# Attention and a quantized convolution block: steps of issue moved, x of the first image on three queues, the constants' transfers behind it

## The chip, the cores and the metric

The kernel runs on one core of a Trainium2 chip. A core has a matrix engine (TensorE, PE in the profile; its weight loads are shown as PEld), a vector engine (VectorE, DVE), a scalar engine (ScalarE, ACT), GpSimd (POOL) and a queue engine (SyncE, SP). Each works through its own list of instructions in order and waits on semaphores for the others. Transfers (DMA) are issued by SyncE, ScalarE or GpSimd, each through its own queue. The metric is the time on the device in microseconds, the median of several runs. Before the change it is 2569.15 us (three runs: 2565.08, 2569.15 and 2569.88).

## The reference

Two layers, on x of four images, each of 128 channels and 64 x 64 points, in float32.

```python
# layer 0: attention over the 4096 points of an image, 4 heads of 32 channels
x_norm = _group_norm(x, norm_w, norm_b)          # 8 groups of 16 channels
qkv = einsum('oc,bchw->bohw', qkv_w, x_norm) + qkv_b
attn = softmax(einsum('bhid,bhjd->bhij', q, k) * 32 ** -0.5)
out = einsum('bhij,bhjd->bhid', attn, v)
x = x + einsum('oc,bchw->bohw', proj_w, out) + proj_b
# layer 1: two 3x3 convolutions with weights quantized to 3 bits
out = relu(batchnorm(conv3x3(x, lsq_quantize(w1, alpha1)), gamma1, beta1))
out = batchnorm(conv3x3(out, lsq_quantize(w2, alpha2)), gamma2, beta2)
x = relu(out + x)
```

The batch norms take mean and variance over all four images.

## The kernel before, in words

`_fast_body` does the work (a second, general path runs only if a bound on the softmax is broken, and it isn't run here).

*Start.* GpSimd fills a few small tiles and issues the loads of all constants (`column`, L95, and L115 to L127). x of the first image comes in eight chunks of 512 points on SyncE's and ScalarE's queues in turn (L590). Meanwhile `keep_warm` gives TensorE products that nobody reads. VectorE takes statistics of each chunk in order (`bn_stats`, L597); `norm_parts` turns them into the scale and the biases of the group norm, in steps zero to eight, with more `keep_warm` between. Then k, q and v of the first chunks are projected (L616). k and q are split into a high and a low part (`kst`, `qst`). Chunk 0 goes straight to its place (`direct`), the others are written to DRAM (`kd`, `qd`) and loaded again in the layout that the scores want (`load_k`, `load_q`).

*Attention.* There are 32 blocks: four images (b), eight blocks of 512 queries each (qb); n counts them all. A block runs over 32 steps kt of 128 keys, each in two halves. `scores` makes a half step of products (L442) and their exponential on ScalarE (L444) into a tile p; `weights` multiplies p with v into acc (L456) and VectorE adds p to a running sum r (L471). In six of the 32 steps (MOVED) the addition is done instead by a transfer of GpSimd's queue that adds into rm (L466), and at the end `merge` adds rm to r (L492). TensorE does three halves of scores, then three of weights, and so on (end of the attention, `run_scores` and `run_weights`). There are nine tiles for p, nine for k, three pairs of banks for scores and two banks for all else (acc, projections, sums).

*Side work.* Everything else is put between these halves by `schedule(n, before)`. It gives every piece a place: `at_half(p, f)` runs f after half p of the block, `add(kt, f)` after step kt, and `visit(i, first, second, evacuate)` uses the i-th end of a group of three (`ends[i]`), where TensorE changes from weights to scores. The place sets the order in each engine's list, not a time: an engine whose list has nothing else left runs ahead. Side work is: the end of the block before (`merge`; `sums` of r over the partitions; `spread`, `invert` and `gather`, which bring the sums to 16 columns, invert them and bring them back as rc by way of DRAM on SyncE's queue; `residual`, which loads x; `weigh`, which multiplies; `project`; `store`); the projections of chunks (in block 0 the rest of k and v of the first image and q of chunk 1, in block 1 the rest of q, later those of the next image); statistics and norm of the next image (`late`); the loads of the next k, v and q; and the quantization of the weights in `pieces`, whose first one of each third is a load on SyncE's queue.

*Convolutions.* The images are cut into bands of 16 rows. `load_band` loads one with its border, `split_band` makes its high and low part (L573, L574), `conv` takes 18 products for each half band. The first two bands are done while the last block is finished. `layer` runs over the bands and calls `prepare(m)` after band m, which is `first` in the first layer: it loads band m + 3 and splits band m + 2. The quantized weights of the second layer wait in DRAM (wqd) and are loaded into raw_w at L808, then copied at band 6.

Of the kernel before, what the change touches and what calls it, by code (L numbers as in the profile page):

```python
# [16 lines left out]
F32 = mybir.dt.float32  # L17
# [5 lines left out]
P = 128  # L23
# [55 lines left out]
def _fast_body(ctx, tc, x, norm_w, norm_b, qkv_wt, qkv_b, proj_wt, proj_b,  # L79
               w1, alpha1, gamma1, beta1, w2, alpha2, gamma2, beta2, out, cnt):  # L80
    nc = tc.nc
# [10 lines left out]
    const = ctx.enter_context(tc.tile_pool(name="const", bufs=1))  # L92
    small = ctx.enter_context(tc.tile_pool(name="small", bufs=2))

    def column(v, name):  # L95
        t = const.tile([P, 1], F32, name=name)
        nc.gpsimd.dma_start(out=t, in_=v.rearrange("(c o) -> c o", o=1))
        return t


# [11 lines left out]
    nc.gpsimd.memset(ones, 1.0)  # L112
    worst = const.tile([P, FB // D], F32, name="worst")
    nc.gpsimd.memset(worst, 0.0)
    nw, nb = column(norm_w, "nw"), column(norm_b, "nb")  # L115
    wqkv = const.tile([P, 3 * P], F32, name="wqkv")
    nc.gpsimd.dma_start(out=wqkv, in_=qkv_wt)
    bkq = const.tile([P, 2], F32, name="bkq")
    nc.gpsimd.dma_start(out=bkq[:, 0:1], in_=qkv_b[P : 2 * P].rearrange("(c o) -> c o", o=1))
    nc.gpsimd.dma_start(out=bkq[:, 1:2], in_=qkv_b[0:P].rearrange("(c o) -> c o", o=1))  # L120
    bv = const.tile([P, P], F32, name="bv")
    nc.gpsimd.dma_start(out=bv, in_=qkv_b[2 * P : 3 * P].partition_broadcast(P))
    wp = const.tile([P, P], F32, name="wp")
    nc.gpsimd.dma_start(out=wp, in_=proj_wt)
    bp = column(proj_b, "bp")
    bn = [(column(gamma1, "gamma1"), column(beta1, "beta1")),
          (column(gamma2, "gamma2"), column(beta2, "beta2"))]  # L127
# [102 lines left out]
    def x_chunk(b, j):  # L230
        return x[b].rearrange("c h w -> c (h w)")[:, j * FB : (j + 1) * FB]
# [74 lines left out]
    def keep_warm(count):  # L306

        t = psa.tile([P, FB], F32, name=f"idle{count}", tag="a")
        for _ in range(count):
            nc.tensor.matmul(t[:, 0:P], gavg, gavg, start=True, stop=True)  # L310
# [276 lines left out]

    halves = [ppool.tile([P, HEADS, FB], F32, name=f"xh{i}", tag="p") for i in range(2)]
    for j in range(NB):
        eng = (nc.sync, nc.scalar)[j % 2]  # L590
        eng.dma_start(out=halves[j // 4][:, j % 4, :], in_=x_chunk(0, j))
    table = const.tile([P, 1], F32, name="table")
    nc.scalar.activation(table, mhalf, AF.Exp)
    keep_warm(26)
    st = small.tile([P, NB, 6], F32, name="st0", tag="st")
    for j in range(NB):
        nc.vector.bn_stats(st[:, j, :], halves[j // 4][:, j % 4, :])  # L597
# [16 lines left out]
        load_v(b, j)  # L614

    for what, j in (("k", 0), ("q", 0), ("k", 1), ("v", 0), ("k", 2), ("v", 1), ("k", 3), ("v", 2),  # L616
                    ("v", 3)):
        for f in first_chunk(j, what, True):
            f()
        if what == "q":  # L620
            five_v()
            six_v()
        if what == "v" and j < 3:
            load_k(0, j + 1)


# [3 lines left out]
    def fetch(b, j):  # L630
        xin[b, j] = load_x(b, j)

    def schedule(n, before):
        b, qb = blocks[n]
        todo = []
        ends = [p for p in range(2 * NK - 2) if (2 * n * NK + p) % 3 == 2]
        two = b + 1 < B and qb in ((3, 4, 5) if b == 0 else (2, 3))

        def at_half(p, f):
            todo.append((p, f))  # L640

        def add(kt, f):
            todo.append((2 * kt + 1, f))

        def visit(i, first, second, evacuate=None, split=True):
            at_half(ends[i], first)
            e = ends[i + 1 if split else i]
            at_half(e, second)  # L650
            if evacuate:
                at_half(e + 1, evacuate)
            return e

        if before:
            add(1, before["merge"])
            e = visit(5 if two else 4 if n == 1 else 6, lambda: before["sums"](0), lambda: before["sums"](1),
                      split=not two and n != 1)
            at_half(e + 2, before["spread"])
            at_half(e + 6, before["invert"])  # L660
            at_half(e + 8, before["gather"])
            at_half(e + 12, before["residual"])
            at_half(ends[18] - 4, before["weigh"])
            at_half(ends[18], before["project"])
            at_half(ends[18] + 2, before["store"])
        if n + 1 < len(blocks):
            add(24 if n == 0 else 14, lambda: load_q(*blocks[n + 1]))
        if n == 0:
            for i, what, j in ((0, "k", 4), (2, "k", 5), (4, "v", 4), (6, "k", 6), (8, "v", 5),
                               (10, "k", 7), (12, "q", 1), (14, "v", 6), (16, "v", 7)):  # L670
                visit(i, *first_chunk(j, what, False), split=False)
                if what == "k":
                    at_half(ends[i] + 5, lambda j=j: load_k(0, j))
        if n == 0:
            for j in (2, 3):
                add(25 + j, lambda j=j: fetch(0, j))
        if n == 1:
            for i, j in zip((0, 2, 8, 10, 12, 14), range(2, NB)):
                if j > 3:
                    at_half(ends[i - 3], lambda j=j: fetch(0, j))  # L680
                visit(i, *project_parts(0, j, lambda j=j: xin[0, j])["q"], split=False)
        qn = qb if b else qb - 1
        if b + 1 < B:
            if qn == 1:
                st = small.tile([P, NB, 6], F32, name=f"st{b + 1}", tag="st")
                for j in range(NB):
                    add(3 * j // 2, lambda j=j: fetch(b + 1, j))
                    add(3 * j // 2 + 3, lambda j=j: nc.vector.bn_stats(st[:, j, :], xin[b + 1, j]))
                late[b] = norm_parts(b + 1, st)
                add(15, late[b][0])  # L690
                for i in (0, 1):
                    at_half(ends[13 + 2 * i], late[b][1 + 2 * i])
                    at_half(ends[13 + 2 * i] + 3, late[b][2 + 2 * i])
            if qn == 2:
                at_half(ends[1], late[b][5])
                at_half(ends[1] + 1, late[b][6])
                at_half(ends[1] + 1, late[b][7])
                at_half(ends[1] + 4, late[b][8])
            if b == 0:
                chunks = {2: (), 3: (0, 1), 4: (2, 3), 5: (4, 5), 6: (6,), 7: (7,)}  # L700
            else:
                chunks = {1: (), 2: (0, 1), 3: (2, 3), 4: (4,), 5: (5,), 6: (6,), 7: (7,)}
            for i, j in enumerate(chunks.get(qb, ())):
                p = project_parts(b + 1, j, lambda j=j: xin[b + 1, j])
                if not two:
                    for what, i in dict(k=1, q=10, v=13).items():
                        visit(i, *p[what])
                    continue
                for what, e in (dict(k=2, q=7, v=9) if i == 0 else dict(k=11, q=13, v=15)).items():
                    visit(e, *p[what], split=False)  # L710
                if i == 1:
                    add(8, lambda j=j: fetch(b + 1, j))
            if qn > 0 and qb + 1 in chunks:
                add(22, lambda j=chunks[qb + 1][0]: fetch(b + 1, j))
            if qb == NB - 1:
                for j in range(NB - 1):
                    add(4 * j + 1, lambda j=j: load_kv(b + 1, j))
        if b > 0 and qb == 0:
            add(1, lambda: load_kv(b, NB - 1))


        if b == B - 1 and qb < NB - 1:
            for kt in (1, 10, 20):
                add(kt, lambda: next(pieces, None))
        elif 0 < b and qb == 0:
            for kt in (1, 10, 15, 20, 25) + ((29,) if b == 1 else ()):
                add(kt, lambda: next(pieces))
        if n == len(blocks) - 1:
            add(5, lambda: load_band(0, 0))
            add(13, lambda: split_band(0, 0))  # L730
            add(17, lambda: load_band(0, 1))
            add(24, lambda: split_band(0, 1))
            add(27, lambda: load_band(0, 2))
        return sorted(todo, key=lambda t: t[0])
# [58 lines left out]
    last["residual"]()  # L793
    conv(ready[0, 0, 0], early[0][:, 1, :], 1, wq[0])
    split_band(*bandlist[2])
    last["sums_at_once"]()
    conv(ready[0, 0, 1], early[1][:, 0, :], 0, wq[0])
    conv(ready[0, 0, 1], early[1][:, 1, :], 1, wq[0])
# [6 lines left out]
    cv = [mid.tile([P, N], F32, name=f"cv{b}") for b in range(B)]  # L805
    raw_w = mid.tile([P, TAPS, P], F32, name="raw_w")
    wq.append(mid.tile([P, TAPS, P], F32R, name="wq1"))
    nc.sync.dma_start(out=raw_w, in_=wqd)  # L808


    a_q, a_g, a_n = ([small.tile([P, 1], F32, name=f"{n}{i}") for i in range(2)]
# [60 lines left out]
    def first(m):  # L872
        if m == 5:
            count_bad()
        if m == 6:
            nc.vector.tensor_copy(wq[1], raw_w)
        if m + 3 < len(bandlist):
            load_band(*bandlist[m + 3])
        if m + 2 < len(bandlist) and m > 0:
            split_band(*bandlist[m + 2])  # L880
# [527 lines left out]
```

## Time and profile before

| engine | busy us | share of the span |
|---|---|---|
| PE | 2515.2 | 98% |
| PEld (overlaps PE) | 1504.3 | 59% |
| DVE | 2137.1 | 83% |
| ACT | 2086.7 | 81% |
| POOL | 282.9 | 11% |

The span of the profiled run is 2567.4 us. The first product of the attention's scores begins at 28.50, the last of acc ends with the copy at 2250.84, the first convolution runs from 2250.7 to about 2396, the second to about 2540, and some 25 us are left for the last normalization and the stores. In a timeline a line gives start, length, engine, line of the kernel, operation, output <- inputs, shapes, count, and in brackets the idle time of the engine before it with what ended it.

### The profile page before, as it was taken

How to read it: one execution, taken by the hardware profiler on the slowest of the kernel's cores; microseconds unless marked ns; L12 is line 12 of the kernel's file. 1: busy time of each engine (PE TensorE's matmuls, PEld its weight loads, DVE VectorE, ACT ScalarE, POOL GpSimd, SP SyncE). 2: the span in 40 equal slices, each digit the busy share in tenths (PEclk: the TensorE clock that was granted, in tenths of full speed). 3: DMA queues.
4: the chain of work that ended last, by engine and by line, in shares of the span. 5: the costliest groups of instructions: out<-in, count | busy, mean ns of one | idle time of the engine just before them, and what ended most of it. 6: DMA issues, size and time to landing. Idle time of an engine off the chain costs nothing.

```text
span 2567.4 us, 65010 instructions
## 1 busy us (share of the span) xinstructions
PE 2515.2 (98%) x28696; PEld 1504.3 (59%) x28696; DVE 2137.1 (83%) x1402; ACT 2086.7 (81%) x2278; POOL 282.9 (11%) x462
## 2 busy tenths in 40 slices
PE   8999999999999999999999999999999999999995
PEld 6555555555555555555555555555555555567774
DVE  5889888889988898889988988889999999954345
ACT  5889888998988899999988999989999999911224
POOL 2111111111011111110111111111000011000000
PEclk9999999999999999999999999999999999999997
DMA  6777667688766776797767667896666667645004
GB/s 179 179 187 164 171 176 180 158 202 188 176 151 174 169 167 155 167 222 172 169 167 175 154 154 165 194 202 149 148 137 143 145 147 149 143 87 162 1 1 165
DMA packets 148825, 403.85 MB, mean 157 GB/s; under 512 B 59416, under 2 KB 60184, under 8 KB 119992
## 3 DMA queue, kind: packets, MB, share of 16 engines
q0 software_dynamic: 45984, 280.92, 47.8%
q1 hardware_dynamic: 100680, 113.07, 17.3%
q10 hardware_dynamic: 1872, 5.64, 0.6%
q8 instruction: 227, 3.72, 0.6%
q14 instruction: 62, 0.51, 0.1%
HBM read 107.48 MB, written 56.42 MB: 64 GB/s over the span
## 4 chain that ended last, share of the span: by engine, by line
PE 85%; DMA 6%; issue 4%; DVE 3%; ACT 1%; SPq 0%; POOL 0%; ACTq 0%; POOLq 0%; DVEq 0%
PE s L442 38%; PE acc L456 34%; PE c L781 8%; DMA rm<-p 3%; DVE r L471 2%; PE pk L317 1%; PE l L488 1%; PE po L317 1%; PE pq L317 1%; PE pv L317 1%; DMA t<-y 1%; ACT p L444 1%; DMA rd<-rq 0%; ACT res L946 0%; DMA x<-in_x_dram 0%
## 5 line engine op out<-in xcount | busy, mean ns | idle before, releaser
L444 ACT ACTIVATE p<-s 128x1024 f32<-128x1024 f32 x2048 | 1949.6, 1032 | 216.0 <-PE s L442 161.4
L471 DVE TENSOR_TENSOR r<-r,p 128x2048 f32<-128x2048 f32 x768 | 1758.2, 2289 | 69.4 <-ACT p L444 18.7
L442 PE MATMUL s<-q,k 64*128 64x512 f32 x8192 | 1140.6, 409 | 6.7 <-ACT p L444 5.5
L456 PE MATMUL acc<-p,v 128*32 128x256 f32 x16384 | 1027.1, 383 | 1.0 <-DVE v L371 1.0
L442 PEld LDWEIGHTS s<-q,k 64*128 64x128 f32 x8192 | 715.1, 185 | 417.4 <-issue 167.7
L456 PEld LDWEIGHTS acc<-p,v 128*32 128x32 f32 x16384 | 462.6, 109 | 485.6 <-issue 249.2
L466 POOL DMA_DIRECT2D rm<-p x160 | 139.1, 870 | 848.0 <-ACT p L444 602.7
L848 ACT COPY cv<-c 128x512 f32<-128x512 f32 x60 | 35.2, 587 | 204.1 <-DVE st L847 204.1
L781 PE MATMUL c<-hi,wq 128*128 128x512 f32 x540 | 140.4, 404 | 3.8 <-DVE hi L573 2.5
L781 PE MATMUL c<-lo,wq 128*128 128x512 f32 x540 | 138.6, 401 | 0.0
L847 DVE BATCH_NORM_STATS2 st<-c 128x6 f32<-128x512 f32 x60 | 41.9, 699 | 103.1 <-PE c L781 82.8
L781 PEld LDWEIGHTS c<-hi,wq 128*128 128x128 f32 x540 | 102.2, 190 | 33.4 <-issue 5.0
L781 PEld LDWEIGHTS c<-lo,wq 128*128 128x128 f32 x540 | 101.6, 188 | 27.2
L352 DVE SCALAR_TENSOR_TENSOR kst<-pk,b,kst 128x512 fp32r<-128x512 f32 x32 | 24.0, 750 | 81.3 <-PE s L442 54.9
L469 DVE TENSOR_TENSOR r<-p,p 128x2048 f32<-128x2048 f32 x32 | 73.2, 2288 | 14.9 <-ACT p L444 14.9
L352 DVE SCALAR_TENSOR_TENSOR qst<-pq,b,qst 128x512 fp32r<-128x512 f32 x32 | 24.0, 751 | 71.9 <-PE s L442 59.7
L356 POOL DMA_DIRECT2D qd<-qst x31 | 23.1, 744 | 277.3 <-DVE qst L352 271.1
L492 POOL DMA_DIRECT2D r<-rm x31 | 26.2, 846 | 214.5 <-DMA rm<-p 100.1
L356 POOL DMA_DIRECT2D kd<-kst x28 | 20.8, 744 | 200.1 <-DVE kst L352 189.9
L488 PE MATMUL l<-r,ones 128*32 128x256 f32 (+1 forms) x504 | 37.7, 383 | 0.7 <-DMA r<-rm 0.7
L351 ACT ACTIVATE kst<-pk,b 128x512 fp32r<-128x512 f32 x32 | 22.3, 700 | 18.4 <-PE pk L317 18.4
L317 PE MATMUL pq<-x,wn 128*32 128x256 f32 x480 | 33.3, 379 | 3.9 <-DMA x<-in_x_dram 2.9
(149 smaller groups left out, 725.7 us busy)
## 6 DMA issues: line engine op xcount, KB each, us to landing
rm<-p POOLq DMA_DIRECT2D x192, 1024.0 KB, 7.6
q<-qd SPq DMA_DIRECT2D x248, 128.0 KB
r<-rm POOLq DMA_DIRECT2D x31, 1024.0 KB, 7.6
x<-in_x_dram SPq DMA_DIRECT2D x86, 256.0 KB
k<-kd SPq DMA_DIRECT2D x124, 128.0 KB
qd<-qst POOLq DMA_DIRECT2D x31, 512.0 KB, 7.5
kd<-kst POOLq DMA_DIRECT2D x28, 512.0 KB, 3.8
y<-x POOLq DMA_DIRECT2D x32, 256.0 KB, 7.1
```

What stands on the lines that cost most here:

```text
L317: nc.tensor.matmul(out[cs, :], w[:, cs], x, start=True, stop=True)
L352: nc.vector.scalar_tensor_tensor(lo, ps[what], bias, t[:, 0, :], ALU.add, ALU.subtract)
L356: (nc.sync if start else nc.gpsimd).dma_start(out=dst[b, j].rearrange("s p n -> p s n"), in_=t)
L442: nc.tensor.matmul(s[:, i, :], k[r, half, c0 : c0 + P], q[r, half, part, :], start=(part == 0), stop=(part == 1))
L444: nc.scalar.activation(pts[step][:, 2 * half : 2 * half + 2, :], s, AF.Exp, scale=SCALE)
L456: nc.tensor.matmul(acc[n][h * D : (h + 1) * D, cs], v[:, kt % KB, h * D : (h + 1) * D], pt[:, h, cs], start=(kt == 0 and half == 0), stop= ...
L466: nc.gpsimd.dma_start(out=msum[n], in_=pt, accum_op=ALU.add)
L469: nc.vector.tensor_tensor(rsum[n], pts[step - 1], pt, ALU.add)
L471: nc.vector.tensor_tensor(rsum[n], rsum[n], pt, ALU.add)
L488: nc.tensor.matmul(t["l"][h * D : (h + 1) * D, cs], ones, r[:, h, cs], start=first, stop=end)
L781: nc.tensor.matmul(ps.rearrange("p (r w) -> p r w", w=W), w[:, tap, :], part[:, r0 + kh : r0 + kh + RB, kw : kw + W], start=(n == 0), stop ...
L847: nc.vector.bn_stats(st[:, b * NB + c, :], ps[:, j, :])
```

## The change

Pieces of the side work get other places, and so other places in the queues.

- The constants' loads are collected (`fill`) and issued by GpSimd after x; the weights come first among them. x's chunks go to GpSimd, SyncE and ScalarE in turn. The first `keep_warm` does 32 products instead of 26, to hold TensorE busy until the statistics are there.
- k of chunk 4 is projected before block 0, and the other projections of block 0 move up. Block 1's projections and their loads of x are moved, so that none meets a buffer or a load that isn't ready; its sums come one place later.
- `invert`, and above all `gather`, come later, behind `residual`, so that SyncE's queue need not stand and wait for the inverted sums.
- At the change of image, the bias of v (`late[b][8]`) comes earlier and k's projection one place later; the last loads of k and v and the weights' pieces come later in the first block.
- Band 3 of the first convolution is loaded earlier, and raw_w after it.

```diff
     def column(v, name):
         t = const.tile([P, 1], F32, name=name)
-        nc.gpsimd.dma_start(out=t, in_=v.rearrange("(c o) -> c o", o=1))
+        fill(t, v.rearrange("(c o) -> c o", o=1))
         return t
...
     for j in range(NB):
-        eng = (nc.sync, nc.scalar)[j % 2]
+        eng = (nc.gpsimd, nc.sync, nc.scalar)[j % 3]
         eng.dma_start(out=halves[j // 4][:, j % 4, :], in_=x_chunk(0, j))
+    for f in transfers:
+        f()
...
-    keep_warm(26)
+    keep_warm(32)
...
     for what, j in (("k", 0), ("q", 0), ("k", 1), ("v", 0), ("k", 2), ("v", 1), ("k", 3), ("v", 2),
-                    ("v", 3)):
+                    ("k", 4), ("v", 3)):
...
-        if what == "v" and j < 3:
+        if what == "v":
             load_k(0, j + 1)
...
-            e = visit(5 if two else 4 if n == 1 else 6, lambda: before["sums"](0), lambda: before["sums"](1),
+            e = visit(5 if two or n == 1 else 6, lambda: before["sums"](0), lambda: before["sums"](1),
                       split=not two and n != 1)
             at_half(e + 2, before["spread"])
-            at_half(e + 6, before["invert"])
-            at_half(e + 8, before["gather"])
+            at_half(e + 8, before["invert"])
             at_half(e + 12, before["residual"])
+            at_half(e + 15, before["gather"])
...
-            add(24 if n == 0 else 14, lambda: load_q(*blocks[n + 1]))
+            add(22 if n == 0 else 14, lambda: load_q(*blocks[n + 1]))
         if n == 0:
-            for i, what, j in ((0, "k", 4), (2, "k", 5), (4, "v", 4), (6, "k", 6), (8, "v", 5),
-                               (10, "k", 7), (12, "q", 1), (14, "v", 6), (16, "v", 7)):
+            for i, what, j in ((0, "k", 5), (2, "v", 4), (4, "k", 6), (6, "v", 5), (8, "k", 7),
+                               (10, "q", 1), (12, "v", 6), (14, "v", 7)):
...
-            for i, j in zip((0, 2, 8, 10, 12, 14), range(2, NB)):
+            for i, j in zip((1, 3, 8, 10, 12, 14), range(2, NB)):
                 if j > 3:
-                    at_half(ends[i - 3], lambda j=j: fetch(0, j))
+                    at_half(ends[i - 5], lambda j=j: fetch(0, j))
...
-                at_half(ends[1] + 4, late[b][8])
+                at_half(ends[1] + 2, late[b][8])
...
-                for what, e in (dict(k=2, q=7, v=9) if i == 0 else dict(k=11, q=13, v=15)).items():
+                for what, e in (dict(k=3, q=7, v=9) if i == 0 else dict(k=11, q=13, v=15)).items():
...
         if b > 0 and qb == 0:
-            add(1, lambda: load_kv(b, NB - 1))
+            add(9, lambda: load_k(b, NB - 1))
+            add(16, lambda: load_v(b, NB - 1))
...
-            for kt in (1, 10, 20):
+            for kt in (3, 11, 21):
                 add(kt, lambda: next(pieces, None))
         elif 0 < b and qb == 0:
-            for kt in (1, 10, 15, 20, 25) + ((29,) if b == 1 else ()):
+            for kt in (3, 12, 17, 22, 26) + ((29,) if b == 1 else ()):
...
     split_band(*bandlist[2])
+    load_band(*bandlist[3])
     last["sums_at_once"]()
...
-    nc.sync.dma_start(out=raw_w, in_=wqd)
...
+        if m == 2:
+            nc.sync.dma_start(out=raw_w, in_=wqd)
         if m == 6:
             nc.vector.tensor_copy(wq[1], raw_w)
-        if m + 3 < len(bandlist):
+        if 0 < m < len(bandlist) - 3:
             load_band(*bandlist[m + 3])
```

More of the change, by code (lines that the diff above doesn't have):

```diff
@@ L93, in _fast_body, with fill @@
     small = ctx.enter_context(tc.tile_pool(name="small", bufs=2))
+    transfers = []
+    def fill(t, src):
+        transfers.append(lambda: nc.gpsimd.dma_start(out=t, in_=src))
     def column(v, name):
         t = const.tile([P, 1], F32, name=name)
-        nc.gpsimd.dma_start(out=t, in_=v.rearrange("(c o) -> c o", o=1))
+        fill(t, v.rearrange("(c o) -> c o", o=1))
         return t
@@ L114, in _fast_body @@
     nc.gpsimd.memset(worst, 0.0)
+    wqkv = const.tile([P, 3 * P], F32, name="wqkv")
+    fill(wqkv, qkv_wt)
     nw, nb = column(norm_w, "nw"), column(norm_b, "nb")
-    wqkv = const.tile([P, 3 * P], F32, name="wqkv")
-    nc.gpsimd.dma_start(out=wqkv, in_=qkv_wt)
     bkq = const.tile([P, 2], F32, name="bkq")
-    nc.gpsimd.dma_start(out=bkq[:, 0:1], in_=qkv_b[P : 2 * P].rearrange("(c o) -> c o", o=1))
-    nc.gpsimd.dma_start(out=bkq[:, 1:2], in_=qkv_b[0:P].rearrange("(c o) -> c o", o=1))
+    fill(bkq[:, 0:1], qkv_b[P : 2 * P].rearrange("(c o) -> c o", o=1))
+    fill(bkq[:, 1:2], qkv_b[0:P].rearrange("(c o) -> c o", o=1))
     bv = const.tile([P, P], F32, name="bv")
-    nc.gpsimd.dma_start(out=bv, in_=qkv_b[2 * P : 3 * P].partition_broadcast(P))
+    fill(bv, qkv_b[2 * P : 3 * P].partition_broadcast(P))
     wp = const.tile([P, P], F32, name="wp")
-    nc.gpsimd.dma_start(out=wp, in_=proj_wt)
+    fill(wp, proj_wt)
     bp = column(proj_b, "bp")
```

## The prediction

> **What bounds the kernel now.** I read the page first, then the timeline of TensorE in each stage, then the timelines of the queues around each place where TensorE stood still.
>
> ```profile
> span 2567.4 us, 65010 instructions
> PE 2515.2 (98%) x28696; PEld 1504.3 (59%) x28696; DVE 2137.1 (83%) x1402; ACT 2086.7 (81%) x2278; POOL 282.9 (11%) x462
> PE 85%; DMA 6%; issue 4%; DVE 3%; ACT 1%; SPq 0%; POOL 0%; ACTq 0%; POOLq 0%; DVEq 0%
> ```
>
> TensorE is the bound: busy for 98% of the span and 85% of the chain that ended last. The change touches no product of TensorE but the warm-up, so all it can win is time in which TensorE stands still or runs slow. That is 2567.4 - 2515.2 = 52 us; 25 of it is the tail after the last matmul, which the change leaves alone, 2 us is the start. About 24 us of idle are spread over the rest. Busy time by stretch shows where:
>
> ```profile
> 100.00:166.00 66.00, 61.32 (x764) 34.58 (x762) 49.67 (x29) 54.95 (x62) 7.91 (x10) 1.00 0.73 183
> 1684.00:1750.00 66.00, 62.93 (x752) 35.60 (x750) 54.41 (x31) 55.94 (x62) 6.71 (x9) 0.97 0.88 205
> 1816.00:1882.00 66.00, 66.00 (x798) 37.47 (x800) 61.40 (x44) 61.59 (x67) 6.19 (x8) 1.00 0.66 144
> 2278.00:2344.00 66.00, 63.49 (x262) 49.58 (x261) 30.76 (x38) 9.40 (x16) 1.60 (x20) 0.97 0.51 96
> ```
>
> The columns are the stretch, its length, busy PE, PEld, DVE, ACT, POOL, then TensorE's clock, DMA share, GB/s. A steady block (1816 to 1882) is full; block 1 (100 to 166) lacks 4.7 us, the start of the fourth image (1684 to 1750) lacks 3.1 and has a clock of 0.97, the first convolution lacks 2.5, again with 0.97. Single places, from TensorE's timeline (in brackets its idle time before the group, and what ended it):
>
> ```profile
> 12.45 0.59 PE L254 MATMUL gm<-mv,gavg 128*128 128x1 f32 x2 [2.82 <-DVE mv L249]
> ...
> 90.70 1.50 PE L456 MATMUL acc<-p,v 128*32 128x256 f32 x24 [1.01 <-DVE v L371]
> ...
> 109.28 1.07 PE L317 MATMUL pq<-x,wn 128*32 128x256 f32 x16 [1.06 <-ACT av L481]
> ...
> 124.08 1.07 PE L488 MATMUL l<-r,ones 128*32 128x256 f32 x16 [0.75 <-DMA r<-rm]
> ...
> 146.84 1.07 PE L317 MATMUL pq<-x,wn 128*32 128x256 f32 x16 [2.67 <-DMA x<-in_x_dram]
> ...
> 750.28 1.07 PE L317 MATMUL pk<-x,wn 128*32 128x256 f32 x16 [1.04 <-DVE bvn L296]
> ...
> 1728.95 2.14 PE L442 MATMUL s<-q,k 64*128 64x512 f32 x8 [3.07 <-ACT p L444]
> ...
> 2282.52 3.71 PE L781 MATMUL c<-hi,wq 128*128 128x512 f32 x9 [2.51 <-DVE hi L573]
> ```
>
> Each of these waits is touched by one of the edits. The last two cost more than their idle time. In the group at 2282.52 nine matmuls took 3.71 us where the next nine took 2.32: the granted clock was 0.5 from 2282.1 to 2285.5. It was 0.5 from 1729.1 to 1732.6 too, and from 12.2 to 19.1.
>
> **What the Trainium skill says.** "TensorE: Matmul & The Clock Gate", What's actually happening: idleness drops TensorE to half clock for windows of some 3.4 us, activity restores it. The trace agrees: stretches of 3.4 and 6.8 us at 0.5, after 2.5 to 3.1 us of idleness; 2.67 us at 144 left the clock at 1, so not each such gap is punished. "DMA: Bandwidth & Descriptors", Issuing engines are not separate DMA queues: issuing on several engines saves issue time alone, the transfers share the same DMA engines. The trace agrees for the two queues of now: after 1.8 us of issues x still arrives until 10.7, bound by bytes. Same page, Anatomy of one DMA: some 2 us are fixed for a transfer issued by GpSimd. Here small ones took 2.2 to 2.5 us when x had come in, but the first (nw, issued at 1.92) landed at 9.36, 7.4 us later, in the thick of x's transfers.
>
> **The change part by part.**
>
> *Start.* Chunks 0, 3 and 6 of x move to GpSimd's queue, and all constants behind them. Bn_stats run in order, eight at about 0.65 us, the first at 4.83 now, the last ending at 11.99, with waits of 0.74 and 1.20 for late chunks. GpSimd issues only after its memsets, at 1.9 instead of 0.8. With no constants in the way and five chunks of 256 KB on the fast queues, those five should be in by 6; chunk 0 is the unknown. If it behaves as a lone transfer it lands at 1.92 + 2.2 = 4.1, near now; if as nw did, at 9.4. I take 6.2: then 6.2 + 8 x 0.65 = 11.4, against 12.0, some 0.6 earlier, but discount it to 0.2 (ends: +1.2 and -2.7). The warm-up of 32 instead of 26 adds 12 matmul instructions of 0.11 us, so it ends at 11.0 instead of 9.6; the idle gap shrinks from 2.8 to 1.2 us and the half clock from 12.2 on should start later or not at all. The nine idle matmuls before the projections (1.63 + 2.91 us at half clock) partly stand in the way of gv and gb: 1.3 us. The constants are needed from 15.7 on and were in at 12.0; issued some 2 us later they still make it, and GpSimd's pow at 15.1, now behind the last constants, too. Start: 1.5 us (ends -0.8, +3).
>
> *Chunk 4 of k before the blocks.* One projection (1.05 us) leaves block 0 and falls into the time in which TensorE waits for q<-qst until 30.0 (1.00 us idle at 28.99 and 0.86 for DVE's v before). Its write to DRAM joins SyncE's queue behind that of chunk 3, well before it is used. Gain 1.05.
>
> *Block 0.* The remaining chunks move two places up; v's chunk 6 comes 6 halves (6 us) earlier, so the 1.01 us at 90.70 go. Gain 1.0.
>
> *Block 1.* q's first chunk leaves the place where it waits for av (1.06), the sums go one place back (0.75; three us more for a merge that landed at 123.9), and x is fetched two places sooner. The 2.67 us: x of chunk 5 stood in SyncE's queue behind rc, which waited for rd to land (issue 132.28, rc at 139.33), so x left at 140.05 only. In the new order it is ahead of rd. The next x again waits for a slot, but three places before use. Sum 4.48; I take 4.4.
>
> *All blocks.* invert goes two halves and the gather of rc seven halves later, after the residual's load. DVE's weigh reads rc at 50 to 58 us into a block, and rc left at 35 us or so, when rd had landed. So rc hardly leaves later than now, and SyncE no longer stands 5 to 7 us before it. By itself this is worth nothing on TensorE: steady blocks have no idle to win, and DVE was never idle before its weigh.
>
> *Handing over to the next image.* bvn is evacuated two halves sooner and k starts one place later: the 1.04 us at 750.28 go; the other two images show no such gap. Gain 1.0.
>
> *First block of an image.* p's buffers are held by the rm<-p transfers: one of 12.01 us (issued at 1715.49, landed 1727.50) kept ACT for 3.96 us and TensorE for 3.07, plus half clock after it: block 24 took 73.3 us where 27 and 30 took 68.3, so 5.0 in all. The same at 1163 (0.85) and 615 (0.34). The kv load (k 512 KB, v 256 KB) and the weights' 192 KB ran beside it. They are now called for at steps 9, 16 and 3 of the block. But a queue runs ahead of the place at which its transfer is called for: SyncE is empty there, and in the new order of its queue only the weights stand ahead of k, so k will leave about as early as now. Only v, behind the sums' small transfers, really moves. 1.2 MB beside rm made 7 us into 12, so 256 KB less is 1.0 us; with some of the half clock, 1.5 for block 24, 0.8 for the other two. Gain 2.3 (ends 0 and 7).
>
> *Convolution.* The load of band 3 was issued at 2275.18, behind raw_w, which waits for the attention's last store (landed 2274.67). It moves ahead, to about 2256, and raw_w to the third band. Band 3 is then split when it is wanted at 2280. Gain 2.51 + (3.71 - 2.31) = 3.9. raw_w is needed four bands later, so nothing queues behind it.
>
> *New waits.* Thirty changes of order will hardly all be free: -1.0 (ends 0 and -4).
>
> Sum: 1.5 + 1.05 + 1.0 + 4.4 + 1.0 + 2.3 + 3.9 - 1.0 = 14.15; 2569.15 - 14.15 = 2555.0 us.
>
> **The rivals.**
> - *Only the waits with one cause go* (k's chunk, block 0, block 1, the handing over, the convolution: 11.35), the start and rm give nothing, and new waits take 3: -8.3, 2560.8 us. For it: DMA's share is 0.88 around 1700, and every byte is still moved. Against: the half clock at the start is a gap that six more matmuls bridge.
> - *The waits move on*: block 1's x waits again, for a slot or in the traffic (rm took 14.2 us there at 144), and DVE, busy 83%, turns up at the places vacated. Left are the convolution and k's chunk, less one: -4, 2565 us. Against it: DVE has slack in block 1 (49.7 of 66).
> - *Slower*: chunk 0 lands as late as nw did (+2.6), and transfers pushed later meet rm within a block, with one more gap and half clock of 5 us at each of the three changes of image (+15), against the 11.35: +6, 2575 us. Against it: moved bytes are 256 KB for each image, in stretches with a DMA share of 0.66.
>
> **How the numbers follow.** Forecast 0.64, one cause only 0.22, moved on 0.09, slower 0.05. The range: the upper bounds of the start and of rm (1.5 and 4.7 more) give 2549, rounded to 2548 below; above, the second case with a run's spread of 3 us, 2564. Faster by over 0.2% is below 2564.0: the forecast, most of the second and little of the third, 0.86; the same 0.10; slower 0.04.
>
> **What would show it.** In the new profile: no idle above 0.5 us on pq<-x in block 1 nor on pk after bvn; no wait of c<-hi for band 3, and no stretch at half clock after 2250; one projection of k less in block 0; clock near 1 between 12 and 15; rm<-p at the start of image four landing in some 11 us, with a gap on p left. It is wrong if the first bn_stats begins later than 7, or if acc or po wait for av, l or x in blocks that were full.

## The result, and the profile after

The changed kernel takes 2548.2 us (six runs, 2546.82 to 2552.28), the kernel before 2567.74 us in the same comparison (six runs, 2562.96 to 2569.88): a ratio of 0.9927, 95% interval 0.9915 to 0.994. That is 19.5 us less; the forecast was 14.15 less and 2555.0 us.

The page of the changed kernel: span, busy time by engine, shares of the chain that ended last. (Lines of the attention stand six further down in the changed kernel, so that the scores' L442 is L448 there; those of the convolution up to ten.)

```profile
span 2546.6 us, 65041 instructions
PE 2509.0 (99%) x28708; PEld 1503.7 (59%) x28708; DVE 2136.7 (84%) x1402; ACT 2087.5 (82%) x2278; POOL 283.2 (11%) x464
PE 91%; DMA 3%; issue 2%; DVE 2%; SPq 1%; ACT 1%; POOL 0%; ACTq 0%; POOLq 0%; DVEq 0%
```

Busy PE is 6.2 us less, though the warm-up does more. That fits the half clock that went: before, it was granted for 13.7 us ahead of the tail, which costs up to half of that; after, for none. The rest of the 20.8 us between the two profiles is idle time of PE. The four kinds of stretches shown of before (block 1, start of image four, a steady block, first convolution), at about the same places; only the second lies some 20 us later in its block, so as to hold the one wait that is new, and where it lay before the busy time (64.41) and the clock (1.00) are the same:

```profile
100.00:166.00 66.00, 65.64 (x826) 36.99 (x820) 54.88 (x33) 59.47 (x67) 9.43 (x12) 1.00 0.75 189
1693.00:1759.00 66.00, 64.41 (x768) 36.52 (x768) 62.81 (x37) 59.97 (x65) 6.22 (x8) 1.00 0.78 180
1800.00:1866.00 66.00, 66.00 (x800) 37.51 (x796) 61.33 (x43) 61.58 (x67) 6.19 (x8) 1.00 0.61 136
2260.00:2326.00 66.00, 66.00 (x279) 51.83 (x278) 32.50 (x42) 10.85 (x19) 1.84 (x22) 1.00 0.45 91
```

Block 1 and the convolution are full and no stretch runs at a lower clock. The second line still lacks 1.6 us, but for a new reason, which TensorE's timeline shows:

```profile
13.12 0.38 PE L260 MATMUL gm<-mv,gavg 128*128 128x1 f32 x2 [1.27 <-DVE mv L255]
...
120.73 1.05 PE L494 MATMUL l<-r,ones 128*32 128x256 f32 x16
...
137.56 1.05 PE L323 MATMUL pq<-x,wn 128*32 128x256 f32 x16
...
1694.72 1.07 PE L323 MATMUL po<-av,wp 128*32 128x512 f32 x8 [1.59 <-DVE av L543]
```

The sums and q's projections of block 1 wait for nothing any more. Instead of p, it is po (the projection of the block before) that waits near 1694, because rc came late.

Stage by stage, measured in the two profiles (a block runs from one copy av<-acc to the next):

| stage | before | after | change | forecast |
|---|---|---|---|---|
| start, to the first exponential (p) | 30.74 | 28.47 | -2.3 | -1.5 |
| rest of block 0 | 77.88 | 76.03 | -1.9 | -2.05 |
| block 1 | 76.55 | 70.93 | -5.6 | -4.4 |
| block 10 (handing over) | 73.16 | 72.07 | -1.1 | -1.0 |
| blocks 7, 8, 15 | 208.47 | 206.40 | -2.1 | -0.8 |
| block 23 | 67.95 | 69.75 | +1.8 | +1.0 for all new waits |
| block 24 | 73.29 | 68.27 | -5.0 | -1.5 |
| block 31 | 63.34 | 62.59 | -0.75 | 0 |
| last copy to the end | 316.56 | 312.66 | -3.9 | -3.9 |

The other 23 blocks agree within 0.3 us each. The first two rows hang together: the changed kernel does one projection more before the scores (k of chunk 4, 1.05 us), which the second row then counts as a gain. And a single profile has its chance in it: block 31 takes 62.6 us in two kernels of experiment 7 too, which change nothing there. The large miss is block 24.

### The profile page after: what moved, and what is told of

Same layout as the page of the kernel before. It is cut to its first block, busy times and chain, and to the rows that moved or that the text cites. A ratio compares the mean times of both kernels' runs of the same rounds, so it can differ in the third digit from the quotient of the medians.

```text
span 2546.6 us, 65041 instructions
## 1 busy us (share of the span) xinstructions
PE 2509.0 (99%) x28708; PEld 1503.7 (59%) x28708; DVE 2136.7 (84%) x1402; ACT 2087.5 (82%) x2278; POOL 283.2 (11%) x464
## 4 chain that ended last, share of the span: by engine, by line
PE 91%; DMA 3%; issue 2%; DVE 2%; SPq 1%; ACT 1%; POOL 0%; ACTq 0%; POOLq 0%; DVEq 0%
PE s L448 40%; PE acc L462 36%; PE c L790 9%; DMA rc<-rd 1%; PE l L494 1%; PE po L323 1%; PE pq L323 1%; PE pk L323 1%; PE pv L323 1%; DVE r L477 1%; DMA q<-qd 1%; ACT p L450 1%; DVE res L956 0%; DMA rm<-p 0%; SPq L428 0%
## 5 line engine op out<-in xcount | busy, mean ns | idle before, releaser
L448 PE MATMUL s<-q,k 64*128 64x512 f32 x8192 | 1138.7, 409 | 1.7 <-ACT p L450 1.3
L448 PEld LDWEIGHTS s<-q,k 64*128 64x128 f32 x8192 | 715.7, 184 | 410.1 <-issue 166.6
L472 POOL DMA_DIRECT2D rm<-p x160 | 139.5, 872 | 801.7 <-ACT p L450 572.4
L470 POOL DMA_DIRECT2D rm<-p x32 | 17.8, 557 | 176.8 <-ACT p L450 108.7
```

Source lines behind the costliest of these rows:

```text
L448: nc.tensor.matmul(s[:, i, :], k[r, half, c0 : c0 + P], q[r, half, part, :], start=(part == 0), stop=(part == 1))
L472: nc.gpsimd.dma_start(out=msum[n], in_=pt, accum_op=ALU.add)
```

## The experiments

Theory at the outset: most edits do what was forecast, but the start gains by the warm-up and the clock, not by x's queues, and block 24 gains by something other than the moved loads of k and v. The rival for the start: x and the constants on their new queues. The rivals for block 24: v out of the way (the forecast), or the place of the gather.

### 1. The warm-up undone

```diff
# of the changed kernel
-    keep_warm(32)
+    keep_warm(26)
```

> The changed kernel with 26 warm-up products again. If the start's gain comes from the clock (the longer warm-up keeps TensorE from a stretch at half clock), the gap before gm grows to some 3.5 us, the clock is 0.5 from about 12 to 19 us, and the scores begin at 30.5 instead of 27.7: 2551 us. If it comes from x and the constants on their new queues, the scores still begin at 27.7 and the time stays 2548 us.

Measured: 2549.83 us (ratio to before 0.9929, 0.9912 to 0.9945), against 2548.2 for the changed kernel (0.9927): in the time, the difference is within the noise. TensorE's timeline of this kernel shows it:

```profile
13.12 0.59 PE L260 MATMUL gm<-mv,gavg 128*128 128x1 f32 x2 [3.16 <-DVE mv L255]
13.56 1.63 PE L316 MATMUL idle<-gavg 128*128 128x128 f32 x6
14.98 0.42 PE L269 MATMUL gv<-dv,gavg 128*128 128x1 f32 x2
15.27 2.91 PE L316 MATMUL idle<-gavg 128*128 128x128 f32 x12
```

gm comes at 13.12 in both, so the data are there at the same time. But here TensorE stood for 3.16 us before it, the clock is 0.5 from 12.9 to 19.8, the twelve idle products take 2.91 us (1.60 in the changed kernel), and the first exponential begins at 30.43 instead of 28.47. The longer warm-up is worth 2.0 us at the start in these two profiles. In five profiled kernels with the changed kernel's start (it, its repeat in 8, the first of 4, and those of 5 and 6) no half clock precedes the scores, and the first exponential begins at 27.66 to 28.70; without the longer warm-up, x on three queues begins as late as the kernel before (30.74).

### 2. The warm-up alone, on the kernel before

```diff
# of the kernel before
-    keep_warm(26)
+    keep_warm(32)
```

> The kernel before with 32 warm-up products, nothing else. If the warm-up keeps the clock, no stretch at half clock before the first scores, which begin at 27.5 to 28 instead of 28.3 to 30.0: 2567 us. If x's and the constants' new queues were needed for it, a stretch at half clock stays and they begin at 28.3 to 30: 2568.5 us.

Measured: 2565.93 us (0.9992, 0.9985 to 0.9999). The start of its timeline, VectorE and TensorE:

```profile
4.66 3.23 DVE L597 BATCH_NORM_STATS2 st<-xh 128x6 f32<-128x512 f32 x5 [4.66 <-DMA xh<-in_x_dram]
8.77 0.69 DVE L597 BATCH_NORM_STATS2 st<-xh 128x6 f32<-128x512 f32 x1 [0.89 <-DMA xh<-in_x_dram]
10.48 1.29 DVE L597 BATCH_NORM_STATS2 st<-xh 128x6 f32<-128x512 f32 x2 [1.02 <-DMA xh<-in_x_dram]
12.23 0.38 PE L254 MATMUL gm<-mv,gavg 128*128 128x1 f32 x2 [0.63 <-DVE mv L249]
12.47 0.91 PE L310 MATMUL idle<-gavg 128*128 128x128 f32 x6
13.45 1.60 PE L310 MATMUL idle<-gavg 128*128 128x128 f32 x12
```

No half clock at the start, and the first exponential begins at 26.47, earlier than in the changed kernel (28.47). So the warm-up is the whole gain of the start and more. Of the 2.0 us between these two, x's new queues lose 0.9: the last statistics end at 12.66 in the changed kernel and at 11.77 here. About as much is the projection that the changed kernel does more before the scores. At the end of block 0, where that is counted in both, the two stand at 104.50 and 104.73 (before: 108.62). In the median only 1.8 us are left of the warm-up's gain. The profiles say why it varies: four profiled kernels with the start of before (before, the second of 4 and the two of 7 below) begin at 30.74, 29.33, 29.64 and 29.03, their half clock lasting 6.8 us once and 3.4 us in the others. The Trainium skill, "TensorE: Matmul & The Clock Gate", What's actually happening, has the window free-running: it doesn't start anew with the kernel. The clock's records agree: wherever a run has several drops, they start whole multiples of one stretch apart (before: 12.245, 1729.149 and 2282.109 us, with stretches of 3.413 us: 503.0 and 162.0 times). So it is likely that the place of a gap in the window decides, though no run here moved a gap alone. Where the page wants an idle window of some 3.4 us for a drop, the runs differ: a gap of 1.95 us was enough (experiment 3).

### 3. Where x stands on GpSimd's queue

```diff
# of the changed kernel; first version (GpSimd's chunks last)
-        eng = (nc.gpsimd, nc.sync, nc.scalar)[j % 3]
+        eng = nc.gpsimd if j > 4 else (nc.sync, nc.scalar)[j % 2]
...
-    keep_warm(32)
+    keep_warm(26)
# second version (two queues)
-        eng = (nc.gpsimd, nc.sync, nc.scalar)[j % 3]
+        eng = (nc.sync, nc.scalar)[j % 2]
```

> The changed kernel with GpSimd's three chunks of x last (5, 6, 7) instead of 0, 3, 6, and 26 warm-up products. If chunk 0 on GpSimd's queue is what delays the statistics (they begin at 7.8), they begin at 4 to 5 us here and end at 10 to 10.3, when GpSimd's last chunk is in; the gap before gm is under 1.5 us, the clock stays at 1, and the scores begin at 25.3: 2546 us. If the arrival of x is bound by bytes alone, the statistics still end near 12.5 and the scores begin at 27.7 or later.

> The changed kernel with x on SyncE's and ScalarE's queues alone, as before the change, the constants behind on GpSimd's, and 26 warm-up products. If GpSimd's queue only delays x, all eight chunks are in by 8 to 9 us, the statistics run from 4.8 to about 10 us and the scores begin at 25 us, no later than with GpSimd's chunks last: 2545.5 us. If a third queue brings x in sooner, the statistics end later than 10.5 us and the scores begin after 25.6.

Measured: GpSimd's chunks last 2545.91 us (0.9916, 0.99 to 0.9933), two queues 2548.63 us (0.993, 0.9913 to 0.9946). In the changed kernel, the eight statistics run without a gap, but late:

```profile
7.82 4.84 DVE L605 BATCH_NORM_STATS2 st<-xh 128x6 f32<-128x512 f32 x8 [7.82 <-DMA xh<-in_x_dram]
```

With GpSimd's chunks last:

```profile
4.80 2.60 DVE L605 BATCH_NORM_STATS2 st<-xh 128x6 f32<-128x512 f32 x4 [4.80 <-DMA xh<-in_x_dram]
7.62 0.70 DVE L605 BATCH_NORM_STATS2 st<-xh 128x6 f32<-128x512 f32 x1 [0.22 <-DMA xh<-in_x_dram]
8.50 1.99 DVE L605 BATCH_NORM_STATS2 st<-xh 128x6 f32<-128x512 f32 x3 [0.18 <-DMA xh<-in_x_dram]
10.95 0.38 PE L260 MATMUL gm<-mv,gavg 128*128 128x1 f32 x2 [0.27 <-DVE mv L255]
```

Chunk 0 is what everything waits for in the changed kernel: issued by GpSimd at 1.92, it landed at 7.80. Put last, GpSimd's chunks hardly hold up the statistics, and the first exponential begins at 26.29. Two queues alone didn't do as well: the last chunks came late (waits of 0.73 and 0.53 us), the statistics ended at 11.00 instead of 10.49, gm came after a gap of 1.95 us, the clock fell to half for 3.4 us, and the first exponential began at 28.15. That looks as if a third queue helped, but the two kernels differ in the constants too. On two queues nothing stands ahead of the constants on GpSimd's queue, and 0.33 MB of them moved before the last of x was in (9.2 us); with GpSimd's chunks last they stand behind x. All queues together had moved 2.43 MB by 9.2 us on two queues and 2.28 MB on three, so the third brought no more bytes, and the constants in x's way may be the whole 0.5 us. The two were not told apart. Shown is only that what is needed first shouldn't be on GpSimd's queue.

### 4. The gather's place

First the changed kernel with the old place, then the kernel before with the new one.

```diff
# of the changed kernel
-            at_half(e + 8, before["invert"])
+            at_half(e + 6, before["invert"])
+            at_half(e + 8, before["gather"])
             at_half(e + 12, before["residual"])
-            at_half(e + 15, before["gather"])
```

> The changed kernel with invert and gather at their old places (e + 6, e + 8, ahead of the residual's load). If the gather behind k's load of chunk 4 is what makes po wait for 1.59 us in block 23, that wait goes and block 23 takes 68 us; if the moved load of k and v is what freed the start of image four, block 24 stays at 68.3 us: 2546.5 us. If it was the gather's place that freed it, ACT waits some 4 us for rm there again and block 24 takes 73 us: 2551 us.

> The kernel before with invert at e + 8 and gather at e + 15, behind the residual's load, and nothing else. If SyncE, standing before the gather, bundles q's load with rm<-p and so keeps p's buffers, this edit alone ends the wait of ACT for rm at the start of image four: block 24 takes 68.3 instead of 73.3 us, blocks 7, 15 and 31 lose 1.1, 1.3 and 0.8 us, block 23 gains a wait of po (1.6 us); and x of chunk 5 no longer waits behind rc, so block 1 loses 2.7 us: 2558 to 2560 us. If the other edits had to come with it, block 24 stays over 71 us and the time over 2563 us.

Measured: 2554.65 us (0.9951, 0.9935 to 0.9968) for the first, 6.5 us over the changed kernel (from separate comparisons, whose intervals just overlap); 2560.76 us (0.9973, 0.9963 to 0.9983) for the second, 7.7 us under before's 2568.5. The timeline of the first, where image four starts:

```profile
1716.83 3.78 ACT L450 ACTIVATE p<-s 128x1024 f32<-128x1024 f32 x4 [3.53 <-DMA rm<-p]
1717.29 0.83 POOL L498 DMA_DIRECT2D r<-rm  x1 [11.46 <-DMA rm<-p]
1717.91 2.14 PE L448 MATMUL s<-q,k 64*128 64x512 f32 x8 [2.65 <-ACT p L450]
```

That is the wait of the kernel before, back again: block 24 takes 72.8 us, though the loads of k and v are at their new places. In the second kernel it is gone (68.28), though they are at their old ones. The other blocks moved as expected: 7 and 15 by -1.1 and -1.8 us, and po's wait appears in block 23 (1.13 us). (Block 31 moved by -0.75, but that is the chance noted above.) Only block 1 didn't: it lost 1.25 us, not 2.7, since the wait for x made way for one of 1.77 us that ends with DVE's r.

Why it does this is seen in SyncE's timeline of block 23. Before:

```profile
1679.21 0.34 SPq L529 DMA_DIRECT2D rd<-rq  x1
1679.64 2.81 SPq L411 DMA_DIRECT2D k<-kd  x4
1682.57 1.25 SPq L415 DMA_DIRECT2D v<-vd  x1
1683.91 1.17 SPq L534 DMA_DIRECT2D rc<-rd  x1
1685.13 10.40 SPq L422 DMA_DIRECT2D q<-qd  x8
```

After:

```profile
1666.48 0.34 SPq L535 DMA_DIRECT2D rd<-rq  x1
1666.88 9.22 SPq L428 DMA_DIRECT2D q<-qd  x8
1676.14 0.43 SPq L241 DMA_DIRECT2D x<-in_x_dram  x1
1676.66 2.35 SPq L417 DMA_DIRECT2D k<-kd  x4
1679.25 0.34 SPq L421 DMA_DIRECT2D v<-vd  x1
1679.78 0.55 SPq L540 DMA_DIRECT2D rc<-rd  x1
```

Before, q's eight loads (1 MB) begin 36.5 us into the block (1685.13 - 1648.61) and run beside rm<-p of step 19, which GpSimd issues at 41.5 us. After, they begin at 31.4 us and the last is issued at 40.3, before that rm<-p. It took 13.9 us before, 11.6 after (13.5 to 14.8 in the six profiled kernels with the old place in this block, 10.9 to 12.3 in the eight with the new one). The rm<-p of a block wait for each other, so those of steps 24 and 28 follow later or sooner: the last landed 10.9 us after the block's end before (7.3 after). While it runs, it holds a buffer of p. Over the 14 profiled kernels the length of block 24 follows this landing: 68.3 us where it comes up to 7.3 us after the block's end, 68.9 at 8.1, 70.3 at 9.2 (the kernel of experiment 2), 72.7 at 10.2, 74.1 at 12.0. So block 24 varies by itself with the old place, from 70.3 to 74.1.

The price is rc, which stands behind the loads of k and v: issued at 1679.78, it landed at 1693.97, and po waited. This wait is also a part of the gain: counted from the start of block 23, the last rm<-p landed only 1.8 us sooner (after 77.1 instead of 78.9 us), and the other 1.8 us are block 23 made longer by po. Together blocks 23 and 24 gain 3.2 us, not 5.0.

### 5. The gather's place in the last blocks of the images alone

```diff
# of the changed kernel
-            at_half(e + 8, before["invert"])
+            end = qb == NB - 1 and b + 1 < B
+            at_half(e + (6 if end else 8), before["invert"])
+            if end:
+                at_half(e + 8, before["gather"])
             at_half(e + 12, before["residual"])
-            at_half(e + 15, before["gather"])
+            if not end:
+                at_half(e + 15, before["gather"])
```

> The changed kernel with invert and gather at their old places in the last block of the first three images alone, where k and v of the next image are loaded. If what matters is that q's load there leaves ahead of the gather, before the fourth rm<-p, then rm<-p of step 19 takes 14 us again, block 24 takes 73 us and po's wait in block 23 goes: 2551 to 2553 us. If it is the order in the other blocks, block 24 stays at 68.3: 2546.5 us.

Measured: 2552.96 us (0.9938, 0.9923 to 0.9953). rm<-p of step 19 takes 14.1 us in block 23, block 24 takes 72.65 us and block 23 67.96. Its place in three blocks of 32 makes 4.8 of the 6.5 us that it is worth in the changed kernel. The other 1.7 us lie within the intervals; in the kernel before, the place also freed 1.25 us in block 1 (experiment 4). Whether it is the later invert or the later gather was not told apart.

### 6. The loads of k and v

```diff
# of the changed kernel
-            add(9, lambda: load_k(b, NB - 1))
-            add(16, lambda: load_v(b, NB - 1))
+            add(1, lambda: load_kv(b, NB - 1))
...
-            for kt in (3, 11, 21):
+            for kt in (1, 10, 20):
...
-            for kt in (3, 12, 17, 22, 26) + ((29,) if b == 1 else ()):
+            for kt in (1, 10, 15, 20, 25) + ((29,) if b == 1 else ()):
```

> The changed kernel with the last load of k and v and the weights' pieces at their old places. If that move (v's 256 KB out of the way of rm<-p) freed the start of image four, block 24 goes back to 71 to 73 us with a wait of ACT for rm of 2 to 4 us: 2551 to 2553 us. If it was the gather, block 24 stays at 68.3 us: 2548 us.

Measured: 2548.47 us (0.9926, 0.991 to 0.9943), as the changed kernel. Block 24 takes 68.93 us instead of 68.27: the move of k and v (with the weights' pieces) is worth 0.7 us there and nothing that shows elsewhere.

### 7. Block 1 and the convolution, each alone

```diff
# of the kernel before; block 1
-            e = visit(5 if two else 4 if n == 1 else 6, lambda: before["sums"](0), lambda: before["sums"](1),
+            e = visit(5 if two or n == 1 else 6, lambda: before["sums"](0), lambda: before["sums"](1),
...
-            for i, j in zip((0, 2, 8, 10, 12, 14), range(2, NB)):
+            for i, j in zip((1, 3, 8, 10, 12, 14), range(2, NB)):
                 if j > 3:
-                    at_half(ends[i - 3], lambda j=j: fetch(0, j))
+                    at_half(ends[i - 5], lambda j=j: fetch(0, j))
# of the kernel before; convolution
     split_band(*bandlist[2])
+    load_band(*bandlist[3])
...
-    nc.sync.dma_start(out=raw_w, in_=wqd)
...
+        if m == 2:
+            nc.sync.dma_start(out=raw_w, in_=wqd)
         if m == 6:
             nc.vector.tensor_copy(wq[1], raw_w)
-        if m + 3 < len(bandlist):
+        if 0 < m < len(bandlist) - 3:
```

> The kernel before with block 1's edits alone (q's first chunks and sums one place back, x fetched two places sooner; gather at its old place). If the places in block 1 make its gain, the waits for av, r and x go and block 1 takes 71 instead of 76.6 us, all else stays: 2562 us. If the gather's place frees x, the wait for x of 2.7 us stays and block 1 takes 73.5 to 74 us: 2564.5 us.

> The kernel before with band 3 loaded earlier and raw_w behind it, nothing else. If raw_w's place in SyncE's queue made band 3 late, the wait of 2.51 us and the half clock after it go: 316.6 us from the last copy of acc to the end become 312.7: 2563.5 us. If other parts of the change help there, a wait is left and it takes over 314 us.

Measured: block 1 alone 2562.08 us (0.9974, 0.9965 to 0.9984), block 1 takes 71.01 instead of 76.55 us; the convolution alone 2564.12 us (0.9984, 0.9977 to 0.9991), 312.90 us from the last copy to the end instead of 316.56. Both are the forecast's mechanism, with nothing else of the change needed. With the convolution's edit, the fourth band follows at full clock:

```profile
2276.30 2.31 PE L781 MATMUL c<-lo,wq 128*128 128x512 f32 x9
2278.44 2.31 PE L781 MATMUL c<-hi,wq 128*128 128x512 f32 x9
2280.59 2.31 PE L781 MATMUL c<-lo,wq 128*128 128x512 f32 x9
```

### 8. The changed kernel again, and a better one

```diff
# of the changed kernel, with experiment 3's first version
-            at_half(ends[18] - 4, before["weigh"])
-            at_half(ends[18], before["project"])
-            at_half(ends[18] + 2, before["store"])
+            i = 19 if qb == NB - 1 and b + 1 < B else 18
+            at_half(ends[i] - 4, before["weigh"])
+            at_half(ends[i], before["project"])
+            at_half(ends[i] + 2, before["store"])
```

> The changed kernel once more, to compare the last version with it on one chip, and to see what repeats: 2548 us, block 1 at 70.9, block 24 at 68.3, po's wait in block 23 of 1.4 to 1.8 us. The scores begin between 27.1 and 28.7, as the clock's windows fall.

> The changed kernel with GpSimd's chunks of x last, 26 warm-up products, and in the last block of the first three images weigh, project and store three halves later. The start as with GpSimd's chunks last alone (scores at 25.5), and if the late rc is all that made po wait in block 23, the wait of 1.6 us goes and block 23 takes 68 us: 2544 us, 4 under the changed kernel. If po's lateness only moves on (to the store or the first sums of the next block), block 23 or 24 keeps 1 us or more of it: 2545.5 us.

Measured: the changed kernel again 2548.15 us (0.9923, 0.9909 to 0.9936), with 70.96 us in block 1, 68.28 in block 24 and a wait of po of 1.77 us in block 23; so these repeat. The better version takes 2544.24 us (0.9909, 0.9894 to 0.9925): 3.9 us under the changed kernel on the same chip, though the intervals of their ratios overlap. Block 23 takes 67.93 us, but block 24 69.38:

```profile
1709.10 0.73 PE L448 MATMUL s<-q,k 64*128 64x512 f32 x4 [0.37 <-ACT p L450]
```

So of the 1.8 us won in block 23, 1.1 come back in the next block, where TensorE waits for p: the last rm<-p landed 8.5 us after the block's end, so po's wait had given it time. The rest of the gain is the start, where the first exponential begins at 25.32.

## Why the prediction was right, and which steps failed

The time (2548.2) is just inside the range, at its lower end (2548), and the direction and the stages were right. That it stayed inside is in part luck: the low end was the sum with the upper bounds of the start and of rm added, and rm did give its upper bound (7.1 of 7), but for another cause than the one worked out. By its own steps:

- *Start.* 1.5 forecast, 2.3 in the two profiles, so the size was fair, but the working was half wrong. The first bn_stats began at 7.82, later than the 7 named as a sign of error: chunk 0 landed at 7.80, halfway from the 6.2 taken to the bad end of 9.4. The statistics ended 0.7 us later than before, where 0.2 sooner was taken, and the warm-up with the clock gave some 2 where 1.3 was taken (experiments 1 to 3). The gap before gm was forecast as 1.2 us and is 1.27, but by two misses that cancel: the warm-up ended at 11.85 instead of 11.0, and gm came at 13.12 instead of about 12.2.
- *Chunk 4 of k, block 0.* 2.05 forecast, 1.9 measured, but the start pays for a part of it, since the projection didn't fall wholly into idle time. From gm to the end of block 0 the gain is 0.4 to 1.5 us where there is no half clock (92.50 in experiment 2, 90.98 to 92.11 in the five profiles named in experiment 1) and 1.5 where both have 6.8 us of it (96.17 before, 94.68 in experiment 1). Not tried alone.
- *Block 1.* 4.4 forecast, 5.6 measured; alone 5.5 (experiment 7). The idle time of the profile (4.66) was right; the rest came off PE's busy time (1.3 us less for the same products). As the ends of matmuls are modelled, that may be waiting too; it isn't shown.
- *Handing over.* 1.0 and 1.1, in block 10, where it was forecast. In the changed kernel's two profiles a wait of gw for DVE (0.52 and 1.03 us) stands in that block now. Not tried alone.
- *All blocks.* Here the prediction failed: "By itself this is worth nothing on TensorE". The gather's place is worth 6.5 to 7.7 us (experiment 4), and 4.8 of the 6.5 lie in three blocks (5). I had looked at who waits for rc, and found nobody, and at SyncE standing, and found it harmless in steady blocks. I had not asked what stands in the queue behind the gather (q's 1 MB) and what it collides with when it is let go (rm<-p of step 19).
- *First block of an image.* 2.3 forecast, 7.1 measured over blocks 7, 8, 15 and 24. The working put it on v's 256 KB; that move gives 0.7 (experiment 6). That k would leave about as early as before was right, and so was the full price of the wait in this profile, idle time plus half clock, of 5.0.
- *Convolution.* 3.9 and 3.9; alone 3.7 (experiment 7).
- *New waits.* One of 1.0 in the sum; one came, of 1.8 us, in block 23. It was the gather's too, in blocks where k and v go ahead of it.

The first rival (only waits with one cause go, the start and rm give nothing) fitted the other steps, but on rm the opposite came: it gave the most. Where the waits were expected to move on, they did so in block 23 and, in the last version, back to 24.

## What to carry to other kernels

Ask of a moved wait not only who waits for its result, but what stands behind it in its queue and what those transfers will run beside: here a queue that stood and was then let go sent its megabyte into the next one's way. And when a wait goes, look at what its time had been good for: po's wait gave rm<-p 1.8 us. When a gap of TensorE ends in half clock, bridge it with idle products before you speed up what it waits for, and count the slow stretch into the price. With several queues, what is needed first belongs on the one that starts first, and what is needed late behind it.

## What was not expected of the hardware

- GpSimd's queue started late. In all 14 profiled kernels its first transfer was issued at 1.92 and its first packet ran at 5.6 to 6.2 us, some 4 us later; the other two queues issued at 0.81 and their first packets ran at 1.8 and at 2.0 to 2.2. It didn't stand back for them: with x on two queues alone (experiment 3) it began at 6.09, with 0.7 MB of x still to come, and in the changed kernel at 5.97, with 0.13 MB left on them. So it is a slow first start; whether it counts from the issue or from the start of the program isn't told apart, as all issued at the same time. In the changed kernel its chunks of 256 KB landed 5.9, 6.0 and 6.2 us after their issue; small transfers issued after 9.6 us landed in 2.2 to 2.4.
- A gap of some 2 us in front of gm was punished by half clock in one kernel (1.95 us, two queues) and not in others (1.93 us, the changed kernel's second profile, and 2.37 in experiment 5). The 6.8 us at half clock came only after 2.82 and 3.16 us.
